# Layer 0's forward transform on sums and differences of halves, and layer 1 without a hand-written order of issue

## The chip, the cores and the metric

The kernel runs on one NeuronCore of one Trainium2 chip, written in Bass with the Tile framework: pools hand out buffers, a planner sets the waits and, where no order is written by hand, the order of the instructions on each engine. The metric is device time in microseconds; less is better. The engines are called PE (matrix products; PEld is its loading of weights), DVE (vector), ACT (activations), POOL (GpSimd) and SP (it only issues DMAs here). All data are float32. In this kernel each matmul of the source appears as two PE instructions in the profile.

## The reference, cut to what matters

x has 16 images of 16 channels, 256x256. Two layers are added to it one after the other, each behind a group normalization with 8 groups (two channels each).

```python
def _L0_conv_ref(x, ty, tx, weights_pole1, weights_pole2, weights_residue):
    alpha = jnp.fft.fft2(x, axes=(-2, -1))
    ...
    A = 1.0 / (omega1[:, None, None, None] - weights_pole1[None])
    Bm = 1.0 / (omega2[:, None, None, None] - weights_pole2[None])
    S = jnp.einsum('ikpq,oikp,xikq->oxik', weights_residue, A, Bm)
    output_residue1 = jnp.einsum('biox,oxik->bkox', alpha, S)
    C = jnp.einsum('biox,oikp->bikpx', alpha, A)
    D = jnp.einsum('bikpx,xikq->bikpq', C, Bm)
    output_residue2 = jnp.einsum('bikpq,ikpq->bkpq', D, weights_residue)
    x1 = jnp.fft.ifft2(output_residue1, s=(Ny, Nx), axes=(-2, -1)).real
    ...
    return x1 + x2 / Nx / Ny

def _L1_conv_ref(x, W1, b1, Wred, bred, Wspan, bspan, W2, b2, Weca):
    f = mish(conv2d(xs, W1, b1))                  # each channel alone, 1 -> 4 maps, 3x3
    top, bot = (f[:, :, :H2], f[:, :, H2:])
    ker = conv2d(jax.nn.relu(conv2d(bot, Wred, bred)), Wspan, bspan)
    ...
    top_inv = (patches * ker[:, None]).sum(axis=2)  # involution of the upper half
    ...
    out = mish(conv2d(shuffled, W2, b2))          # 64 -> 16 maps, 3x3
    pooled = out.mean(axis=(2, 3))
    ...
    return x * gate[:, :, None, None]

x = x + _L0_conv_ref(_gn(x), ...)
x = x + _L1_conv_ref(_gn(x), ...)
return x
```

## The kernel before

Four stages run one after the other, and only DRAM tensors pass between them.

**Layer 0 forward** (`layer0_forward`, from L69). Tables `at`, `bt` (the poles' transforms), `cr`, `ci` (the residues) are built first (L91 to L139). Then for each image `b`, four groups `cg` of four channels: load 1 MB of pixels as `z`, with row halves `h` side by side (L156), statistics on DVE (`bn_stats`), `group_norm_scalars` (two tiny matmuls with `ones`, a chain of small DVE operations, one square root on ACT), and normalization of `z` in place, half of it on DVE, half on POOL (L171). For each channel and column half `xh`, PE makes the row transform `pu` (L180: frequencies 0 to 131, real and imaginary, 264 columns, two row halves accumulated) and `pv` (L194: the product with the pole table, 192 columns). `pu` is copied to `u` by ACT and DVE (L190, L192), `pv` to `v` by ACT (L201), then four products with `bt` give `pd` (L204), which DVE and POOL gather with the residues into `acc` (L214 to L219). After the four groups, the column transform of the image follows: for 33 groups of four frequencies, four matmuls `px` (L233) of 64 weight columns and 512 moving columns; ACT and DVE copy `px` to `o`, POOL issues the store to `al` (L246), whose layout is [33, 64, image, 2, 256].

**Layer 0 mix** (`layer0_mix`) loads `al` one frequency group at a time (L371, SP queue), builds the transfer function `s` (L424), multiplies it with all images (L443), and transforms back along one axis (L470) to `hd`. **Layer 0 back** (`layer0_back`) finishes the inverse transform (L606), adds it to x, normalizes for layer 1, and writes `xp` and the padded `zn`.

**Layer 1** (`layer1`). An image is cut into nine units (j, h): eight of 30 rows by 8 channels and a tail of 4 channels at a time (`blocks`). A unit does, in the class `Unit`: `lower` (conv1 of the lower half, L740; mish to `bot`, L758), `reduce` (1x1 products `pr`, L768; ReLU to `r`, L776; stores of `bot`), `upper(0)`, `upper(1)` (conv1 of the upper half, 16 mish pieces into `wide`, L788), `spread` (eight POOL copies, L800 and L801), `involution(f)` for four maps f (two matmuls `pd`, L808; DVE products and sums, L816 and L819), and stores of `top`. `conv2` of the image before runs at the same time, 48 matmuls in two halves with one PSUM buffer `c2ps` (L882), each closed by a mish with a running sum (L891). `gate` closes an image (L897 to L920): a sum, a tiny matmul, an exponential on ACT (which needs another function table), and four pieces of output that SP loads (`o`, three buffers), POOL scales and stores. `pr`, `pd` and the gate's product share three PSUM buffers (`psd`); conv1 has two.

Layer 1's order on PE, ACT, DVE and POOL is written by hand: `manual_schedule` takes the instructions as the program gives them. A round i handles the next unit's lower, reduce, upper and spread, and between them this unit's four involutions and the two halves of one conv2; rows for a conv2 are asked for one round ahead (`conv2_rows`):

```python
            if nxt:
                nxt.lower()
            if now:
                now.involution(0)
            next(second, None)
            if nxt:
                nxt.reduce()
            if now:
                now.involution(1)
```

All other stages are ordered by the planner. DMAs of POOL are issued in POOL's queue between its other work, those of SP in SP's.

Of the kernel before, what the change touches and what calls it, by code (L numbers as in the profile page):

```python
# [16 lines left out]
C = 16  # L17
N = 256
# [50 lines left out]
def layer0_forward(ctx, tc, d, al, bd):  # L69


    nc = tc.nc
    nb = d["x"].shape[0]
    cp = ctx.enter_context(tc.tile_pool(name="fc", bufs=1))
    sm = ctx.enter_context(tc.tile_pool(name="fs", bufs=2))
    wx = load(nc, cp, d["wx"], [P, 2, 3, N], "wx")
    wxn = load(nc, cp, d["wxn"], [P, 2, 2, 512], "wxn")
    fy = load(nc, cp, d["fy"], [P, 2, 8 * NF], "fy")
    ones = load(nc, cp, d["ones"], [P, P], "ones")

    at = cp.tile([P, 2, C, 3, 64], F32, name="at")
    bt = cp.tile([P, 2, C, 3, 64], F32, name="bt")

    cr = cp.tile([P, C, P], F32, name="cr")
    ci = cp.tile([P, C, P], F32, name="ci")

    with tc.tile_pool(name="fa", bufs=1) as ap, tc.tile_pool(name="fap", bufs=2, space=PSUM) as pp:
        kcol = load(nc, ap, d["kcol"], [P, 2], "kcol")
        for t, axis, planes in ((at, "1", (1, 0, 2)), (bt, "2", (1, 2, 0))):
# [18 lines left out]
            for y in range(2):  # L108
                for half in range(2):
                    cols = slice(512 * half, 512 * half + 512)  # L110
                    for out, terms in ((0, ((0, 0), (2, 1))), (1, ((0, 1), (1, 0)))):
# [12 lines left out]
                        if out == 0:  # L124
                            nc.scalar.copy(dst[:, :, planes[0]], src)
                        else:
                            nc.scalar.copy(dst[:, :, planes[1]], src)
                            nc.vector.tensor_scalar(dst[:, :, planes[2]], src, -1.0, None, ALU.mult)
        mk = load(nc, ap, d["mk"], [P, C], "mk")
        mkb = mk.unsqueeze(1).unsqueeze(3).to_broadcast([P, C, C, M])  # L130
        for t, name in ((cr, "rr"), (ci, "ri")):
            r = ap.tile([P, C, M], F32, tag="res", name=f"res_{name}")
            for a in range(2):
                nc.sync.dma_start(out=r[64 * a : 64 * a + 64], in_=d[f"{name}_kp"])
            rb = r.unsqueeze(2).to_broadcast([P, C, C, M])
            for part in range(2):
                o = t[:, :, 64 * part : 64 * part + 64].rearrange("p i (k q) -> p i k q", q=M)
                nc.vector.tensor_tensor(o, mkb, rb, ALU.mult)
# [3 lines left out]
    up = ctx.enter_context(tc.tile_pool(name="fu", bufs=1))  # L142
# [4 lines left out]
    psv = ctx.enter_context(tc.tile_pool(name="psv", bufs=1, space=PSUM))  # L147
    psx = ctx.enter_context(tc.tile_pool(name="psx", bufs=2, space=PSUM))

    for b in range(nb):  # L150

        u = up.tile([P, 2, 2, NF, 2, 4, 8], F32, tag="u", name="u")
        acc = dp.tile([P, 4, P], F32, tag="acc", name="acc")
        for cg in range(4):
            z = xp.tile([P, 4, 2, N], F32, tag="z", name="z")
            nc.sync.dma_start(  # L156
                out=z.rearrange("p c h x -> p (c h) x"),
                in_=d["x"][b, 4 * cg : 4 * cg + 4].rearrange("c (h p) x -> p (c h) x", p=P),
            )
            mv = sm.tile([P, 2, 2], F32, tag="mv", name="mv")  # L160
            st = sm.tile([P, 4, 6], F32, tag="st", name="st")
            for c in range(4):
                nc.vector.bn_stats(st[:, c], z[:, c].rearrange("p h x -> p (h x)"))
            for g in range(2):
                nc.vector.bn_aggr(mv[:, g], st[:, 2 * g : 2 * g + 2].rearrange("p c s -> p (c s)"))
            nm = sm.tile([P, 2], F32, tag="nm", name="nm")
            rs = sm.tile([P, 2], F32, tag="rs", name="rs")
            group_norm_scalars(nc, sm, psv, ones, mv, 2, nm, rs)
            for g, eng in ((0, nc.vector), (1, nc.gpsimd)):
                zg = z[:, 2 * g : 2 * g + 2]  # L170
                eng.tensor_scalar(zg, zg, nm[:, g : g + 1], rs[:, g : g + 1], ALU.add, ALU.mult)  # L171
            pd = psv.tile([P, 4, P], F32, tag="pd", name="pd")
            for c in range(4):
                ch = 4 * cg + c
                v = vp.tile([P, 2, 3, 64], F32, tag="v", name="v")
                pv = psv.tile([P, 2, 192], F32, tag="pv", name="pv")
                for xh in range(2):
                    pu = psu.tile([P, 2, 4 * NF], F32, tag="pu", name="pu")
                    for yh in range(2):
                        nc.tensor.matmul(  # L180
                            pu.rearrange("p l f -> p (l f)"),
                            lhsT=z[:, c, yh, P * xh : P * xh + P],
                            rhs=fy[:, yh],
                            start=yh == 0,
                            stop=yh == 1,
                        )
                    dst = u[:, xh, :, :, ch // 8, :, ch % 8]
                    src = pu.rearrange("p l (g f) -> p l g f", f=4)
                    if xh == 0:
                        nc.scalar.copy(dst, src)  # L190
                    else:
                        nc.vector.tensor_copy(dst, src)  # L192
                    for yh in range(2):
                        nc.tensor.matmul(  # L194
                            pv[:, xh],
                            lhsT=z[:, c, yh, P * xh : P * xh + P],
# [966 lines left out]
```

## Time and profile before

| what | value |
|---|---|
| median of 3 runs (lowest, highest) | 11,036.04 us (11,033.31, 11,036.97) |
| the profiled execution: its time, its span | 11,036.97 us, 11,035.1 us |
| forward: first matmul of a group norm, first `pu`, first and last start of `px` | 117.3, 126.1, 200.9, 2,262.4 us |
| mix: first `ps`, last start of `ph` | 2,379.5, 5,652.8 us |
| back: first `py`, last start of `py` | 5,851.5, 6,680.3 us |
| layer 1: first conv1, last `c2ps` | 6,706.6, 11,004.9 us |
| busy in all: PE, DVE, ACT, POOL | 9,866.8, 4,483.4, 3,222.3, 2,977.2 us |
| forward's PE rows: `pu`, `pv`, `pd`, `px` | 562.6, 428.4, 273.6, 969.7 us |
| layer 1's PE rows: `c2ps`, `c`, `pd`, `pr` (full units) | 1,423.0, 1,039.8, 1,024.3, 283.8 us |
| granted PE clock, mean | 0.883 |

A row of the profile names the line, the engine, the operation, what it writes and reads, the shape and the number of instructions; then busy time and the mean of one in ns; then the idle time of the engine ahead of the row and what ended it. For PE, `128*64 128x512` is a weight tile of 128 rows and 64 columns and 512 moving columns. [...] the spacing of starts says what it costs in a stream, and busy time counts overlapping instructions once.

### The profile page before, as it was taken

What the parts mean: (1) busy time and instruction counts of PE and PEld (TensorE: products, weight loads), DVE (VectorE), ACT (ScalarE), POOL (GpSimd) and SP (SyncE); (2) the same over time, 40 slices, a digit from 0 to 9 for tenths busy, and PEclk for the clock granted to TensorE, in tenths of its full rate; (3) what the DMA queues carried; (4) which work ended last, traced back from release to release, by engine and by line L of the source; (5) the groups of instructions that cost most, each with busy time, mean ns of one, the idle gap of its engine ahead of it and who ended that gap; (6) DMA issues with size and microseconds to landing.
All of it is one profiled execution on the core that took longest, in us unless ns stands there. A gap on an engine that the chain in (4) does not pass through costs nothing.

```text
span 11035.1 us, 141924 instructions
## 1 busy us (share of the span) xinstructions
PE 9866.8 (89%) x56576; PEld 5619.0 (51%) x56576; DVE 4483.4 (41%) x7653; ACT 3222.3 (29%) x5154; POOL 2977.2 (27%) x3757
## 2 busy tenths in 40 slices
PE   7999999969999999999948997988888888888887
PEld 4666666647666776677636773322222222222222
DVE  4333333242221222212156665555555555555553
ACT  1111111111111111111110114555555555555553
POOL 1111111111111111111101223444444444444443
PEclk9999999977777777777768998999999999999999
DMA  1222222221222212222208996677777777777776
GB/s 59 63 67 66 64 64 66 55 41 36 45 47 47 40 39 46 47 45 38 42 21 274 325 326 182 196 217 220 221 219 216 212 219 216 213 220 214 215 220 199
DMA packets 985862, 1478.78 MB, mean 134 GB/s; under 512 B 74906, under 2 KB 846294, under 8 KB 953078
## 3 DMA queue, kind: packets, MB, share of 16 engines
q1 hardware_dynamic: 848406, 928.46, 31.6%
q0 software_dynamic: 136800, 541.23, 15.1%
q8 instruction: 453, 7.42, 0.3%
q14 instruction: 203, 1.66, 0.1%
HBM read 860.70 MB, written 608.70 MB: 133 GB/s over the span
## 4 chain that ended last, share of the span: by engine, by line
PE 83%; DMA 5%; DVE 5%; issue 3%; ACT 2%; POOL 1%; SPq 0%; ACTq 0%; POOLq 0%; DVEq 0%
PE pg L443 13%; PE c2ps L882 12%; PE px L233 9%; PE pd L808 8%; PE ph L470 8%; PE c L740 8%; PE ps L424 5%; PE pu L180 4%; PE py L606 4%; PE pv L194 3%; PE py L609 2%; PE pd L204 2%; DMA rows<-cf 2%; PE pr L768 2%; DMA z<-zn 1%
## 5 line engine op out<-in xcount | busy, mean ns | idle before, releaser
L788 ACT ACTIVATE wide<-c,b 32x512 f32<-32x512 f32 x2176 | 1477.4, 679 | 480.6 <-PE c L740 429.4
L882 PE MATMUL c2ps<-rows,c 128*32 128x512 f32 x12288 | 1423.0, 611 | 156.4 <-DMA rows<-cf 142.6
L819 DVE TENSOR_TENSOR top<-pd,t 32x512 f32<-32x512 f32 x2176 | 1504.2, 691 | 52.5
L816 DVE TENSOR_TENSOR t<-pd,r 64x512 f32<-64x512 f32 x1088 | 744.0, 684 | 1817.4 <-PE pd L808 1795.0
L443 PE MATMUL pg<-s,alb 128*64 128x32 f32 x16896 | 1407.2, 350 | 1.7 <-issue 1.7
L443 PEld LDWEIGHTS pg<-s,alb 128*64 128x64 f32 x16896 | 1402.1, 272 | 10.6 <-issue 7.8
L808 PE MATMUL pd<-wide,dw 128*128 128x512 f32 x2048 | 1024.3, 623 | 156.5 <-POOL wide L801 155.4
L740 PE MATMUL c<-z,w 102*128 102x512 f32 x2048 | 1039.8, 639 | 112.2 <-ACT wide L788 89.4
L800 POOL COPY wide<-wide 32x1031 f32<-32x1031 f32 (+1 forms) x576 | 569.0, 988 | 1812.7 <-ACT wide L788 1785.2
L882 PEld LDWEIGHTS c2ps<-rows,c 128*32 128x32 f32 x12288 | 391.1, 111 | 1166.4 <-issue 901.3
L233 PE MATMUL px<-wxn,u 128*64 128x512 f32 x4224 | 969.7, 599 | 0.0
L470 PE MATMUL ph<-ix,yt 128*128 128x512 f32 x2112 | 955.3, 605 | 6.7 <-ACT yt L465 5.9
L488 POOL DMA_DIRECT2D hd<-h x512 | 271.9, 535 | 2338.0 <-ACT h L478 2242.1
L424 PE MATMUL ps<-tt,lt 128*64 128x256 f32 x4224 | 659.0, 423 | 156.5 <-DVE lt L410 123.6
L808 PEld LDWEIGHTS pd<-wide,dw 128*128 128x128 f32 x2048 | 376.6, 195 | 782.6 <-issue 435.5
L740 PEld LDWEIGHTS c<-z,w 102*128 102x128 f32 x2048 | 395.1, 195 | 652.3 <-issue 508.4
L233 PEld LDWEIGHTS px<-wxn,u 128*64 128x64 f32 x4224 | 382.8, 136 | 564.2 <-issue 562.3
L470 PEld LDWEIGHTS ph<-ix,yt 128*128 128x128 f32 x2112 | 395.4, 193 | 517.5 <-issue 435.1
L451 DVE COPY y<-pg 128x512 f32<-128x512 f32 x132 | 116.6, 883 | 1224.2 <-PE pg L443 1224.2
L180 PE MATMUL pu<-fy,z 128*128 128x264 f32 x2048 | 562.6, 399 | 35.6 <-DVE z L171 17.8
L801 POOL COPY wide<-wide 32x1031 f32<-32x1031 f32 (+1 forms) x576 | 572.5, 994 | 36.0
L606 PE MATMUL py<-h,iy 128*128 128x256 f32 x2048 | 541.5, 383 | 1.0 <-DMA h<-hd 1.0
(204 smaller groups left out, 9851.0 us busy)
## 6 DMA issues: line engine op xcount, KB each, us to landing
rows<-cf SPq DMA_DIRECT2D x128, 2176.0 KB
z<-zn SPq DMA_DIRECT2D x768, 256.0 KB
cf<-top POOLq DMA_DIRECT2D x512, 240.0 KB, 6.8
cf<-bot POOLq DMA_DIRECT2D x96, 840.0 KB, 9.2
alb<-al SPq DMA_DIRECT2D x528, 128.0 KB
zn<-zb SPq DMA_DIRECT2D x128, 516.0 KB
z<-in_x SPq DMA_DIRECT2D x64, 1024.0 KB
al<-o POOLq DMA_DIRECT2D x256, 256.0 KB, 3.7
```

What stands on the lines that cost most here:

```text
L180: nc.tensor.matmul(pu.rearrange("p l f -> p (l f)"), lhsT=z[:, c, yh, P * xh : P * xh + P], rhs=fy[:, yh], start=yh == 0, stop=yh == 1,)
L233: nc.tensor.matmul(ps[64 * k : 64 * k + 64], lhsT=u[:, xh, part, g0 + j + k].rearrange("p h f c -> p (h f c)"), rhs=wxn[:, xh, part], star ...
L424: nc.tensor.matmul(ps[64 * h : 64 * h + 64, v], lhsT=lt[:, h, v, k], rhs=tt[:, h, k], start=True, stop=True,)
L443: nc.tensor.matmul(ps[64 * h : 64 * h + J, f], lhsT=alv[:, :, fx], rhs=sv[:, :, fx], start=True, stop=True,)
L470: nc.tensor.matmul(ph, lhsT=yt[:, v, h], rhs=ix[:, h, v], start=n == 0, stop=n == 3,)
L606: nc.tensor.matmul(py[:, yh], lhsT=iy[:, v, ys], rhs=h[:, k, v], start=v == 0, stop=False)
L740: nc.tensor.matmul(ps[:, q], lhsT=w, rhs=cols[:, 1 - q], start=True, stop=True)
L788: nc.scalar.activation(self.feat[64 - 32 * q : 96 - 32 * q, f, self.groups[g], :H], ps[32 * f : 32 * f + 32, q], AF.Mish, bias=b1[0][32 * ...
L808: nc.tensor.matmul(ps, lhsT=dwt if self.tail else dw, rhs=self.feat[:, f, cs, :H], start=True, stop=True,)
L816: nc.vector.tensor_tensor(t[64:128], ps[:64], self.r[:, cs], ALU.mult)
L819: nc.vector.tensor_tensor(self.top[32 * f : 32 * f + 32, cs, q], ps[lanes], t[lanes], ALU.add)
L882: nc.tensor.matmul(ps[32 * j : 32 * j + 32], lhsT=c2[:, blk, dx, :], rhs=t[:, 4 * j + blk : 4 * j + blk + 4, x : x + H], start=(blk, dx) = ...
```

## The change

It has two parts.

**Forward.** A group of four channels becomes a step of a pipeline. `halves(b, cg)` loads and makes statistics as before, but instead of normalizing it forms, with the mean taken out, the sum of the two row halves (`eo[:, 0]`, DVE) and their difference (`eo[:, 1]`, POOL). Even row frequencies need only the sum and odd ones only the difference, so `rows` computes each from 128 rows instead of 256: `pu` and `pv` are 128 columns each, one after the other on the same weights. The same is done with the column halves: ACT copies the right half's `pu`, DVE adds and subtracts (two operations a channel) into `u`, so that `columns` makes even and odd column frequencies from 128 columns each, 256 moving columns instead of 512. The scale of the norm is put in when ACT copies `pv` and `px` (all `px` copies are ACT's). `pd` gathers two channels at a time on 64 partitions each; `finish` folds the halves with six small matmuls (`pair`). `halves` of the next group is called ahead of `rows`, and eight groups of `columns` of the image before after each `rows`; `u` has two fixed buffers. `al` has the layout [33, 2, 64, image, 256], its stores are twice as many and half as long, and its loads in the mix take whole pieces. The tables `fy`, `wxn`, `ix`, `krow_t` are reordered to even before odd.

**Layer 1.** The class and the hand-written order are gone. `unit` does one unit's work in its natural order, `conv2` asks for its own rows and runs whole after it, the stores of `top` come before those of `bot`, and the planner sets the order of all engines.

```diff
+    def halves(b, cg):
...
+        eo = ep.tile([P, 2, 4, N], F32, tag="eo", name="eo")
+        for g in range(2):
+            cs = slice(2 * g, 2 * g + 2)
+            nc.vector.scalar_tensor_tensor(
+                eo[:, 0, cs], z[:, cs, 0], nm2[:, g : g + 1], z[:, cs, 1], ALU.add, ALU.add
             )
+        nc.gpsimd.tensor_tensor(eo[:, 1], z[:, :, 0], z[:, :, 1], ALU.subtract)
+        return eo, rs
+
+    def rows(b, cg, eo, rs, acc):
...
+                        lhs = eo[:, e, 2 * j + a, P * xh : P * xh + P]
                         nc.tensor.matmul(
+                            pu[:, xh, e].rearrange("p v m -> p (v m)"),
+                            lhsT=lhs,
+                            rhs=fy[:, e],
+                            start=True,
+                            stop=True,
+                        )
...
+                            pv[:, a, xh],
+                            lhsT=lhs,
+                            rhs=at[:, e, ch].rearrange("p l m -> p (l m)"),
...
+                nc.scalar.copy(right, pu[:, 1])
+                for h, sign in ((0, ALU.add), (1, ALU.subtract)):
+                    nc.vector.tensor_tensor(
+                        u[:, h, :, :64, :, ch],
+                        pu[:, 0].rearrange("p e v m -> p v m e"),
+                        right.rearrange("p e v m -> p v m e"),
+                        sign,
+                    )
+            vt = vp.tile([P, 2, 2, P], F32, tag="v", name="v")
+            nc.scalar.activation(vt, pv, AF.Copy, scale=rs[:, j : j + 1])
...
                     nc.tensor.matmul(
-                        pd[:, c],
-                        lhsT=v[:, xh, 1 - k : 3 - k].rearrange("p l m -> p (l m)"),
+                        pd[64 * a : 64 * a + 64, j],
+                        lhsT=vt[:, a, xh, 64 * k : 64 * k + 64],
...
+    def columns(b, g0, rsc):
...
                         nc.tensor.matmul(
-                            ps[64 * k : 64 * k + 64],
-                            lhsT=u[:, xh, part, g0 + j + k].rearrange("p h f c -> p (h f c)"),
-                            rhs=wxn[:, xh, part],
-                            start=i == 0,
-                            stop=i == 3,
+                            ps[64 * k : 64 * k + 64, :, h],
+                            lhsT=u[:, h, part, g0 + j + k].rearrange("p f c -> p (f c)"),
+                            rhs=wxn[:, h, part],
+                            start=part == 0,
+                            stop=part == 1,
                         )
...
+            for v in range(2):
                 nc.gpsimd.dma_start(
-                    out=al[g0 + k : g0 + n : 2, :, b].rearrange("g p v x -> p g (v x)"),
-                    in_=o[64 * k : 64 * k + 64, :w],
+                    out=al[g0 + k : g0 + n : 2, v, :, b].rearrange("g p x -> p g x"),
+                    in_=o[64 * k : 64 * k + 64, :w, v],
                 )
+
+
+    steps = [(b, cg) for b in range(nb) for cg in range(4)]
+    ready = halves(*steps[0])
+    rsc = None
+    for i, (b, cg) in enumerate(steps):
+        now = ready
+        if i + 1 < len(steps):
+            ready = halves(*steps[i + 1])
+        if cg == 0:
+            acc = dp.tile([P, 2, P], F32, tag="acc", name="acc")
+        rows(b, cg, *now, acc)
+        if b:
+            for g0 in range(8 * cg, 8 * cg + 8 if cg < 3 else NF, 4):
+                columns(b - 1, g0, rsc)
+        if cg == 3:
+            rsc = finish(b, acc)
+    for g0 in range(0, NF, 4):
+        columns(nb - 1, g0, rsc)
...
-                    nc.sync.dma_start(out=alb[p : p + 8, j], in_=al[g, q : q + 8, :, v])
+                    q = 16 * j + 8 * h
+                    nc.sync.dma_start(out=alb[p : p + 8, j], in_=al[g, v, q : q + 8])
...
-    with tc.manual_schedule(engines={E.PE, E.Activation, E.DVE, E.Pool}):
-        begin_unit(0)
-        begin_unit(1)
...
-            if nxt:
-                nxt.lower()
-            if now:
-                now.involution(0)
-            next(second, None)
-            if nxt:
-                nxt.reduce()
...
+    i = 0
+    for b in range(nb + 1):
+        if b:
+            acc = sm.tile([P, 16], F32, tag="acc", name="acc")
+        for s, (j, h) in enumerate(blocks):
+            if b < nb:
+                unit(b, i, j, h)
+                i += 1
             if b and s < 8:
...
+                conv2(b - 1, s, acc)
+        if b:
+            gate(b - 1, acc)
```

## The prediction

> **What bounds the kernel now.** I read the page's first two parts, then busy time by stage (the stretches), then the instruction timeline of one steady piece of each changed stage, and last the waits. All of it says that TensorE (PE) sets the end, in every stage.
>
> ```profile
> PE 9866.8 (89%) x56576; PEld 5619.0 (51%) x56576; DVE 4483.4 (41%) x7653; ACT 3222.3 (29%) x5154; POOL 2977.2 (27%) x3757
> ...
> PE 83%; DMA 5%; DVE 5%; issue 3%; ACT 2%; POOL 1%; SPq 0%; ACTq 0%; POOLq 0%; DVEq 0%
> ```
>
> The stretches (columns: PE, PEld, DVE, ACT, POOL busy, granted clock, DMA share, GB/s): a piece of layer 0's forward stage, the gap after it, a piece of the mix, a piece of layer 1.
>
> ```profile
> 1400.00:2200.00 800.00, 774.07 (x3990) 516.61 (x3989) 248.65 (x618) 140.32 (x270) 152.91 (x174) 0.99 0.23 63
> ...
> 2263.00:2380.00 117.00, 33.19 (x131) 26.88 (x130) 77.02 (x48) 9.95 (x17) 12.90 (x8) 0.65 0.20 37
> ...
> 3000.00:4000.00 1000.00, 950.45 (x7435) 688.30 (x7435) 226.43 (x343) 157.70 (x280) 146.68 (x203) 0.75 0.22 43
> ...
> 8000.00:9000.00 1000.00, 888.95 (x4298) 302.62 (x4302) 538.04 (x802) 524.93 (x782) 440.82 (x571) 0.95 0.71 214
> ```
>
> The forward stage is PE 97% at clock 0.99, other engines under a third: work taken off PE there shortens it. Its size is seen in PE's timeline (start, length, count):
>
> ```profile
> 1000.31 1.07 PE L233 MATMUL px<-wxn,u 128*64 128x512 f32 x2
> 1001.31 1.16 PE L204 MATMUL pd<-bt,v 128*128 128x128 f32 x8
> 1002.40 33.91 PE L233 MATMUL px<-wxn,u 128*64 128x512 f32 x150
> ```
>
> The 150 px follow one another at 33.91/150 = 0.226 us, the 128-column pd at (1.16-0.275)/7 = 0.127. Every matmul of the source is two instructions, each with a weight load.
>
> Layer 1 is one round of 27.88 us per unit (ACT's first r of a round stands at 8307.86, 8335.74, 8363.63), and inside a round PE has no hole over 0.8 us. One line each from the timelines of ACT, POOL and DVE follows one unit from its mish to the first product of its involution; the square brackets hold the idle time before and who ended it:
>
> ```profile
> 8313.46 11.24 ACT L788 ACTIVATE wide<-c,b 32x512 f32<-32x512 f32 x16 [3.09 <-PE c L740]
> ```
> ```profile
> 8319.91 1.03 POOL L800 COPY wide<-wide 32x1031 f32<-32x1031 f32 x1 [15.67 <-ACT wide L788]
> ```
> ```profile
> 8323.33 0.68 DVE L816 TENSOR_TENSOR t<-pd,r 64x512 f32<-64x512 f32 x1 [4.03 <-PE pd L808]
> ```
>
> One unit's own chain is conv1, mish, POOL copies, pd, DVE; with DVE's eight tiles it is longer than a round. It is hidden only because PE works on two units and on conv2 at once. PE's timeline near the end of the kernel shows what a wait costs beyond its length: 24 conv2 calls (48 instructions) take 5.44 us, and 7.10 after PE had stood for 3.03.
>
> ```profile
> 10926.53 7.10 PE L882 MATMUL c2ps<-rows,c 128*32 128x512 f32 x48 [3.03 <-DMA rows<-cf]
> 10934.59 5.44 PE L882 MATMUL c2ps<-rows,c 128*32 128x512 f32 x48 [0.95 <-ACT e L891]
> ```
>
> [...] Here 3.03 us did (7.10 against 5.44), 2.95 us at 10942.98 did not (5.44). [...]
>
> **The change, part 1: forward.** It runs in 64 steps of four channels. PE per step: pu and pv are 64 instructions of 128 columns in place of 264 and 192; nearest rows are pd (0.127) and the 128x128 transposes (8 in 1.05 us, 0.131), so 0.134: 8.6 us. Bounds 0.107 (pv's 192 columns take 0.161 back to back; by columns) and 0.190 (the weight load's own duration). pd: 32 instructions with 64-wide weights, 0.08 from L443 (0.083 apart), bounds 0.067 and 0.137: 2.6. px: 66 on average, 256 columns, 0.12 from L424 (94 in 11.32 us), bounds 0.113 and 0.150: 7.9. Norm matmuls 0.6. Sum 19.7. Before: 2,135 us over 64 steps, 33.4.
>
> Other engines per step. DVE: bn_stats 4x0.68, small norm operations 2.9, the even half 2x0.65 (L105's 1.22 halved), eight u sums of 256 strided elements at 0.60 (L192; bounds 0.41 of L215 and 1.04), pd out 0.9: 12.6, up to 16. ACT: four copies 0.38, two v 0.6, four px 0.6, 5.3. POOL: the odd half 2.5 (twice L219's 1.27 for 512), acc 1.3, 8.5 al DMAs at 0.60 (twice as many), 8.9. None reaches 19.7, so all are hidden under PE; without that cover DVE's 16 would be the bound. The odd half is queued behind the al DMAs, which wait for ACT's last px copies; it is needed a step later, so that costs nothing.
>
> Waits that PE gets: its order puts gn_var after four matmul calls, DVE answers gn_mean with five operations, 0.5 us late; behind gn_var stand all pu. v is read 0.15 and 0.8 late (ACT copies `right` first). [...] So 21.7 a step. The setup keeps its 126 us (fewer table operations, one table loaded twice, in the shade of DVE). 126 + 4 steps without px, held by DVE, x14.5 + 60x21.7 + the last 132 px calls (32) = 1,518 against 2,263: -745. The mix reads al in whole 128 KB pieces; PE waits for that load nowhere now (L443: 1.7 us in all): nothing. al's writes have rows of half the length; DMA share 0.23 leaves room.
>
> **Part 2: layer 1.** The diff takes the order written by hand away and leaves it to the planner. The changed kernel as built has, for each steady unit on PE: lower conv1 (8 instructions), pr, upper conv1, 20 conv2 calls, three pd, then conv2 and single pd in turn, 11 conv2. From the unit's start: lower 0 to 3.6 (0.45 each), second bot ends 4.9 on ACT, its pr 5.9, wide starts 2.06 after the upper conv1 does, 7.96. POOL follows 6.45 later (8313.46 to 8319.91), a pair of copies 2.2: 16.6. PE has done its 20 conv2 (0.227 each) at 14.0: it stands 2.75 us. pd 16.75, DVE 1.17 later, 17.9. psd has three buffers, so the eighth pd waits until DVE has done its fifth tile, 5x2.15 (0.72 for t, 1.43 for two tops): 28.65; pd and sending 1.0, 11 conv2 2.5: 32.15. Against 27.88: +4.3. What else moves is covered. The tops' stores stand on POOL after the unit's copies, now ahead of the bots', and wait for DVE's last tile, 2.95 us into the next unit; with 3.1 of issuing they end at 6.1, and POOL's next copy is not due before 14.4. On SP the rows of a conv2 follow its own unit's z and wait for the conv2 two earlier, so they are issued at the start of the unit before and have a whole round for the 12 to 15 us that they take now (12.70 from 6927.12, 14.77 from 7192.43).
>
> Boundary of a batch. Before: 266.4 a batch (gates at 8499.5 and 8766.0), so 71.2 for tail plus first unit. After, from the tail's first conv1: its last pd 13.6, gate's exponential 19.5, mish's table back 20.9; only then the next bot, whose conv1 was done at 16.8. Rows for the next conv2 wait for the tail's last stores (22, landing 25), then 12 us: 37. SP has them ahead of the fourth o and the next z; z is needed later. 37 conv2 at a cold clock end at 47.9, seven DVE-paced tiles and the next lower at 61.9; that is a unit's start at about 57.5. A batch: 7x32.15 + 57.5 = 282.6, +16.2. Fifteen: +243. Batch 0 has no conv2: 26.75 against 24.4 a unit, +19. The last conv2 start later, +10. Clock: the 2.75 us wait is at the edge; 0 to 1.66 a unit, of which DVE's pace hides a part, 0.3 over 120 units: +35. Sum +307.
>
> Total, against the profiled execution's 11,037.0 (span 11,035.1; the median of the three runs is 11,036.0, the same within 0.01%): 11,037 - 745 + 307 = 10,599.
>
> **The rivals.** (A) Weight loads don't overlap at short streams: 0.190 and 0.137 for all, so 64x0.190 + 98x0.137 + 0.6 = 26.2 a step with the waits hidden under it, 4.5x60 = 270 more than forecast: 10,870. Against: pd's 0.127 with the same weights. (B) Layer 1 loses nothing: the psd waits are absorbed, -745 alone: 10,290. For it: PE's work per round is 26.4 in both. Against: PE's order. (C) Slower: in layer 1 the clock falls at each wait. Place: the pr, pd and e waits of each unit; price 1.66 each. It decides from a unit of 36.1 us, where 15x(8x36.1+25.3-266.4)+29 = 745. Three falls a unit give 37.1: +865, 11,160. Against: 0.8 and 0.95 us waits cool nothing now. That the change does not lessen forward work is excluded by the matmul shapes in its build.
>
> **How the numbers follow.** Forecast 0.66, its own range 10,420 to 10,790 (forward waits 1.5 a step either way 90, boundary 6 a batch 90, clock 0 to 150). A 0.14, B 0.13, C 0.07. The range 10,270 to 10,890 holds the forecast and the better part of A and B. Within 0.2% (22 us, about what a measurement of this kernel can tell from no change) only by accident between A and C: 0.01; slower 0.07; faster 0.92.
>
> **What would show it.** Forward ending near 1,520, PE about 90% busy, pu and pv 0.13 apart; else A. Layer-1 rounds of 32 us, PE waiting 2 to 3 us for POOL before the first pd and idling for DVE before later ones; 28 us would be B. Clock in layer 1 at 0.9 or more; under 0.8 is C. I am wrong if DVE's u sums take over 1.5 us, or if the mix changes.

## The result and the profile after

The changed kernel takes 11,296.31 us (median of 4 runs, 11,290.09 to 11,306.25); the kernel before, run beside it, 11,036.51 us (11,033.31 to 11,037.51). The ratio is 1.0237 (95% interval 1.0219 to 1.0254): 2.4% slower. The forecast was 10,599 us. The profiled execution has a span of 11,304.4 us against 11,035.1, that is +269, and the two traces split it by stage:

| stage, from and to | before | after | difference | forecast |
|---|---|---|---|---|
| start to the last start of `px` | 2,262.8 | 1,370.0 | -893 | -745 |
| last `px` to first `ps` | 116.7 | 110.7 | -6 | 0 |
| mix, first `ps` to last `ph` | 3,273.8 | 3,476.1 | +202 | 0 |
| back with the gaps around it, to the first conv1 | 1,053.3 | 1,053.2 | 0 | 0 |
| layer 1, first conv1 to the end | 4,328.5 | 5,294.4 | +966 | +307 |

The forward stage gave more than was forecast. The mix, for which the forecast had nothing, and layer 1 ate it and more.

The page of the kernel after, its first part and the engines' shares of the chain that ended last:

```profile
PE 9843.9 (87%) x56768; PEld 5331.7 (47%) x56768; DVE 4424.0 (39%) x7953; ACT 3209.6 (28%) x5170; POOL 3142.1 (28%) x4031
...
PE 69%; ACT 10%; DMA 7%; DVE 6%; issue 4%; POOL 4%; SPq 0%; ACTq 0%; POOLq 0%; DVEq 0%
```

PE's busy time is almost what it was (9,866.8), though the forward stage has 815 us less of it (1,318 where 2,133 were). So PE got busier elsewhere at the same number of calls, or spends busy time standing. Its share of the chain fell from 83% to 69%; ACT and DMA have come in. The stretches of the kernel after (PE, PEld, DVE, ACT, POOL busy, granted clock, DMA share, GB/s), one each from forward, mix and layer 1:

```profile
700.00:1300.00 600.00, 600.00 (x5172) 508.31 (x5170) 293.94 (x930) 178.40 (x352) 272.17 (x353) 1.00 0.39 106
2100.00:3100.00 1000.00, 911.73 (x6847) 643.57 (x6845) 211.69 (x321) 149.35 (x267) 139.18 (x194) 0.74 0.22 41
8000.00:9000.00 1000.00, 860.12 (x3410) 241.45 (x3410) 435.74 (x655) 415.54 (x621) 359.26 (x465) 0.93 0.61 174
```

Forward: PE 100% at clock 1.00, nothing else over half. Mix: PE 912 us of 1,000 where it was 950. Layer 1: 3,410 matmul instructions in 1,000 us where there were 4,298, yet PE is still 86% busy, and the clock is 0.93 in the mean (0.95 before). PE does a fifth less there in nearly the same busy time. That is the thing to explain.

**Forward.** PE's timeline inside a step, in the kernel after (start, length, count):

```profile
715.20 0.39 PE L204 MATMUL pu<-fy,eo 128*128 128x128 f32 x2
715.42 0.39 PE L211 MATMUL pv<-at,eo 128*128 128x128 f32 x2
...
717.14 1.58 PE L232 MATMUL pd<-bt,v 128*64 128x128 f32 x16
...
723.89 7.41 PE L288 MATMUL px<-wxn,u 128*64 128x256 f32 x58
```

Read starts, not lengths: two `pu` instructions are 0.39 us long, but to the next two `pv` it is 0.22, so 0.11 each; the 16 `pd` end where the next `pu` starts (718.65), 0.094 each; the 58 `px` run to 731.23, 0.127 each. A step (712.22 to 731.47) is 19.25 us, with no wait in it.

**Layer 1.** The same three marks of one unit as were shown of before, in the timelines of ACT, POOL and DVE of the kernel after:

```profile
8310.91 11.26 ACT L853 ACTIVATE wide<-c,b 32x512 f32<-32x512 f32 x16 [1.36 <-PE c L817]
```
```profile
8317.37 1.03 POOL L863 COPY wide<-wide 32x1031 f32<-32x1031 f32 x1 [8.83 <-ACT wide L853]
```
```profile
8320.72 0.69 DVE L872 TENSOR_TENSOR t<-pd,r 64x512 f32<-64x512 f32 x1 [17.57 <-PE pd L868]
```

The chain from mish to DVE is as long as before (9.8 us, where it was 9.9), but DVE has now been idle for 17.57 us ahead of it: the next unit's front no longer runs beside this unit's back. PE's timeline of the rest of the unit, which starts at 8302.13 and ends at 8339.84, 37.72 us in all where the forecast had 32.15:

```profile
8319.56 4.50 PE L868 MATMUL pd<-wide,dw 128*128 128x512 f32 x6 [2.44 <-POOL wide L864]
8323.99 1.05 PE L934 MATMUL c2ps<-rows,c 128*32 128x512 f32 x2
8324.97 1.13 PE L868 MATMUL pd<-wide,dw 128*128 128x512 f32 x2
8326.02 1.06 PE L934 MATMUL c2ps<-rows,c 128*32 128x512 f32 x6
8328.04 1.05 PE L934 MATMUL c2ps<-rows,c 128*32 128x512 f32 x2 [0.95 <-ACT e L943]
...
8330.07 1.07 PE L934 MATMUL c2ps<-rows,c 128*32 128x512 f32 x8
...
8332.13 1.94 PE L934 MATMUL c2ps<-rows,c 128*32 128x512 f32 x12
...
8335.05 1.05 PE L934 MATMUL c2ps<-rows,c 128*32 128x512 f32 x4
...
8337.09 2.81 PE L934 MATMUL c2ps<-rows,c 128*32 128x512 f32 x22
```

Two instructions are one conv2 call. One call takes 0.98 us to the start of what follows (mostly a `pd`; most of their rows are left out), four 1.00, six 1.87, two 0.99, eleven 2.75; three, ahead of a wait, are 1.06 long. The price goes by fours begun, some 0.95 each, not by calls. In a stream (40 instructions at 8312.54 in 4.57 us) a call is 0.23, four of them 0.91. Four calls in a row write the four groups of 32 output rows (`ps[32 * j : 32 * j + 32]`) with weights of 32 columns each, and run side by side: the stream's first four instructions start from 8312.54 to 8312.56, the next four from 8313.01 to 8313.03 (run 11 shows it for conv2 and `pr`). The planner puts a `pd` (128 weight columns) after 20, 21, 25, 29, 35 and 37 of the unit's 48 calls. A piece that is no multiple of four takes the time of the next whole four: by time the unit has 15 fours, where 48 calls need 12. Over the kernel the same 12,288 instructions are busy for 1,835.7 us, where they were for 1,423.0:

```profile
L934 PE MATMUL c2ps<-rows,c 128*32 128x512 f32 x12288 | 1835.7, 613 | 186.8 <-ACT e L943 174.3
```

A second thing is hidden in the mean of the clock. The first three `pd` of the unit take 4.43 us. Two stretches of 1 us show why (the columns as above; the clock is the last but two):

```profile
8321.00:8322.00 1.00, 1.00 (x2) 0.25 (x1) 0.96 (x2) 0.97 (x2) 0.94 (x2) 0.50 0.26 52
...
8324.00:8325.00 1.00, 1.00 (x4) 0.16 (x3) 0.87 (x2) 0.00 (x0) 0.99 (x1) 1.00 0.00 0
```

From 8320.59, 1 us behind the end of the 2.44 us wait, the granted clock is 0.5 for 3.41 us. The records of the clock have a fall at this place in 104 of 118 full units with a conv2; PE then takes 20.3 us (median) from the first `pd` to the next unit. In four units that had the wait and kept their clock it takes 19.1. So the fall costs 1.2 us a unit, some 125 us in all by an estimate from these figures. In the kernel before, the clock is 1.00 throughout the rounds that the forecast quotes (from 8307.86 to 8363.63).

**Mix.** The costliest group of ACT there and PE's `ph`, in the kernel before and after, then one unit of the mix on ACT and on PE in the kernel after:

```profile
L478 ACT COPY h<-ph 128x512 f32<-128x512 f32 x264 | 154.7, 586 | 847.9 <-PE ph L470 736.0 <-DMA hd<-h 94.5 <-PE pt L459 17.4
L470 PE MATMUL ph<-ix,yt 128*128 128x512 f32 x2112 | 955.3, 605 | 6.7 <-ACT yt L465 5.9 <-DVE yt L467 0.7
```
```profile
L555 ACT COPY h<-ph 128x512 f32<-128x512 f32 x264 | 154.7, 586 | 1050.8 <-PE ph L547 746.1 <-DMA hd<-h 304.7
L547 PE MATMUL ph<-ix,yt 128*128 128x512 f32 x2112 | 1026.0, 639 | 134.6 <-ACT yt L542 133.9 <-DVE yt L544 0.7
```
```profile
2319.90 0.58 ACT L555 COPY h<-ph 128x512 f32<-128x512 f32 x1 [8.74 <-DMA hd<-h]
```
```profile
2320.81 9.23 PE L547 MATMUL ph<-ix,yt 128*128 128x512 f32 x14 [4.30 <-ACT yt L542]
```

ACT waits 305 us in all for a store of `h` to land (94.5 before); `yt` is queued behind that on ACT, and PE's `ph` waits for `yt`: 134 us in the open (5.9 before), while its busy time is 71 longer (1,026.0 against 955.3). That makes 199 of the 202. The records of single transfers show what is new: the loads of `alb` come in pieces of 16 KB that take 1.8 us each (median over the mix), where they were 1 KB and 0.10. Stores of `h`, in pieces of 4 KB and 0.3 us as before, go out in the middle of them: the four issued from 2,295 to 2,310 us landed 16.4 us later (median). Of all 544 such stores 181 took more than 12 us to land, where 19 had before. The others land sooner than before, so the median over all, 3.4 us against 6.7, does not show it.

So the theory was: the three stages add up independently; layer 1 loses by broken fours of conv2, the mix by the new layout of `al`. The rivals: that layer 1's loss comes in part from the new layer 0, that it is the changing between two kinds of matmul that costs, or that DVE or POOL set the round; and for the mix, that the new order of rows or the clock is to blame. The expectations of the runs on layer 1's order do not reckon with the fall of the clock; the traces of runs 6, 7 and 9 have it too, and are read for it there.

### The profile page after: what moved, and what is told of

It reads as the page before. It is cut to its first block, busy times and chain, and to the rows that moved or that the text cites. A ratio compares the mean times of both kernels' runs of the same rounds, so it can differ in the third digit from the quotient of the medians.

```text
span 11304.4 us, 142231 instructions
## 1 busy us (share of the span) xinstructions
PE 9843.9 (87%) x56768; PEld 5331.7 (47%) x56768; DVE 4424.0 (39%) x7953; ACT 3209.6 (28%) x5170; POOL 3142.1 (28%) x4031
## 3 DMA queue, kind: packets, MB, share of 16 engines
q0 software_dynamic: 141152, 541.25, 16.3%
## 4 chain that ended last, share of the span: by engine, by line
PE 69%; ACT 10%; DMA 7%; DVE 6%; issue 4%; POOL 4%; SPq 0%; ACTq 0%; POOLq 0%; DVEq 0%
PE pg L520 12%; PE pd L868 9%; PE c2ps L934 8%; ACT wide L853 8%; PE ph L547 6%; PE c L817 6%; PE ps L501 5%; PE px L288 5%; DMA hd<-h 5%; PE py L683 4%; PE pu L204 2%; PE pr L837 2%; PE py L686 2%; PE pv L211 2%; DMA o<-xp 2%
## 5 line engine op out<-in xcount | busy, mean ns | idle before, releaser
L934 PE MATMUL c2ps<-rows,c 128*32 128x512 f32 x12288 | 1835.7, 613 | 186.8 <-ACT e L943 174.3
L868 PE MATMUL pd<-wide,dw 128*128 128x512 f32 x2048 | 1277.4, 737 | 385.0 <-POOL wide L864 377.8
L547 PE MATMUL ph<-ix,yt 128*128 128x512 f32 x2112 | 1026.0, 639 | 134.6 <-ACT yt L542 133.9
L817 PE MATMUL c<-z,w 102*128 102x512 f32 x2048 | 1026.0, 641 | 22.5 <-DMA z<-zn 22.5
L943 ACT ACTIVATE e<-c2ps,b 128x512 f32<-128x512 f32 x256 | 175.9, 687 | 2151.4 <-PE c2ps L934 2151.0
L547 PEld LDWEIGHTS ph<-ix,yt 128*128 128x128 f32 x2112 | 418.3, 205 | 692.8 <-issue 475.6
L886 POOL DMA_DIRECT2D cf<-top x512 | 257.1, 502 | 1646.8 <-DVE top L875 1619.9
L288 PE MATMUL px<-wxn,u 128*64 128x256 f32 x4224 | 580.3, 386 | 0.0
```

The source lines that it names most:

```text
L288: nc.tensor.matmul(ps[64 * k : 64 * k + 64, :, h], lhsT=u[:, h, part, g0 + j + k].rearrange("p f c -> p (f c)"), rhs=wxn[:, h, part], star ...
L547: nc.tensor.matmul(ph, lhsT=yt[:, v, h], rhs=ix[:, h, v], start=n == 0, stop=n == 3,)
L817: nc.tensor.matmul(ps[:, q], lhsT=w, rhs=cols[:, 1 - q], start=True, stop=True)
L868: nc.tensor.matmul(ps, lhsT=dwt if tail else dw, rhs=feat[:, f, cs, :H], start=True, stop=True)
L934: nc.tensor.matmul(ps[32 * j : 32 * j + 32], lhsT=c2[:, blk, dx, :], rhs=t[:, 4 * j + blk : 4 * j + blk + 4, x : x + H], start=(blk, dx) = ...
```

## The experiments

**1. The new layer 0 alone.** The changed `layer0_forward`, `layer0_mix`, tables and layout, with the function `layer1` of before:

```diff
-            if b < nb:
-                unit(b, i, j, h)
...
+    with tc.manual_schedule(engines={E.PE, E.Activation, E.DVE, E.Pool}):
+        begin_unit(0)
```

> The changed layer 0 (forward, tables, layout of al) with the hand-ordered layer 1 of before. Theory (the parts add up): the traces show the forward 893 us shorter, the mix some 200 us longer and layer 1 966 us longer; without the last, 11,036 - 893 + 200 = about 10,345 us. Rival (part of layer 1's loss comes from what the new layer 0 leaves behind, a lower clock for instance): layer 1 stays longer than its 4,328 us, and the time lies between 10,400 and 11,300.

Measured: 10,358.96 us, ratio 0.9369 (0.9355 to 0.9383). Its mix is 3,496 us long, its layer 1 4,328, exactly as before.

**2. The new layer 1 alone.** The other way round: all of layer 0 as before, and

```diff
-    with tc.manual_schedule(engines={E.PE, E.Activation, E.DVE, E.Pool}):
-        begin_unit(0)
...
+            if b < nb:
+                unit(b, i, j, h)
```

> The layer 0 of before with the changed layer 1 (the order left to the planner). Theory: all of layer 1's loss, about 966 us, so 12,000 us, with a unit's round of 37.7 us instead of 27.9. Rival (part of it belongs to the new layer 0): clearly under 12,000.

Measured: 12,038.01 us, ratio 1.0886 (1.0870 to 1.0902). Layer 1 is 5,308 us (5,294 in the changed kernel), the steady batch 327.7 us (327.5). The parts add up (0.9369 and 1.0886 make 1.0255, against 1.0237); nothing of layer 1's loss belongs to the new layer 0.

**3 and 4. Two cures for the mix**, both on the kernel of run 1. The old layout of `al` under the new arithmetic (the stores of `al` in the forward, left out here, are again half as many and twice as long):

```diff
-    al = dram.tile([NF, 2, 64, nb, N], F32, name="al")
+    al = dram.tile([NF, 64, nb, 2, N], F32, name="al")
...
-                    nc.sync.dma_start(out=alb[p : p + 8, j], in_=al[g, v, q : q + 8])
+                    nc.sync.dma_start(out=alb[p : p + 8, j], in_=al[g, q : q + 8, :, v])
```

> As the kernel with the changed layer 0 and the old layer 1, but al keeps its old layout, frequency by row by image by part, so that each load of alb is 128 pieces of 1 KB again; the arithmetic is the changed one. Theory (the new layout makes the alb loads hold up the hd stores, so h buffers come free late and ACT, yt and ph wait): the mix goes back to some 3,273 us, so 10,140 to 10,160, about 200 below the run with the new layout; ACT's wait for hd falls from some 305 us to under 100. Rival (the mix lost its 200 us elsewhere, by the new order of rows and tables or by a lower clock): no difference, 10,345.

And, with the new layout kept, more buffers for `h`:

```diff
+    hb = ctx.enter_context(tc.tile_pool(name="mhh", bufs=8))
...
-            o = hp.tile([P, 2, N], F32, tag="h", name="h")
+            o = hb.tile([P, 2, N], F32, tag="h", name="h")
```

> As the kernel with the changed layer 0 and the old layer 1, new layout of al kept, but 8 buffers for h in the mix instead of 3. Theory (stores land late, and only the three buffers turn that into a wait): ACT's wait for hd goes and the time falls to about 10,140 to 10,160, as with the old layout, or a little lower since before had 94 us of that wait too. Rival A (the loads hold up something other than the h buffers): no difference to the run with three, 10,345. Rival B (the mix lost its time elsewhere): no difference either, and the run with the old layout does not differ either.

Measured: 10,148.94 us, ratio 0.9178 (0.9163 to 0.9193), and 10,152.26 us, ratio 0.9180 (0.9166 to 0.9194). ACT's row in the first and in the second:

```profile
L554 ACT COPY h<-ph 128x512 f32<-128x512 f32 x264 | 154.8, 586 | 854.6 <-PE ph L546 717.2 <-DMA hd<-h 130.3 <-PE pt L535 7.1
```
```profile
L556 ACT COPY h<-ph 128x512 f32<-128x512 f32 x264 | 154.8, 586 | 822.4 <-PE ph L548 800.6 <-DMA hd<-h 21.8
```

Either cure alone brings the mix back (3,294 and 3,289 us; with the old layer 0, in run 2 beside them, it is 3,294). PE's own wait for `yt` is 5.0 us and nothing. The loss needs both: stores that land late, and only three buffers behind them. The records of the stores agree: over 12 us to land took 23 of them with the old layout, and 201 with eight buffers, where they no longer hold up PE. Order of rows and tables are those of the changed kernel in both runs, so they are not the cause.

**5. Both cures together**, the two diffs above in one kernel.

> The changed forward, al in its old layout, 8 buffers for h in the mix and the hand-ordered layer 1 of before: the two cures of the mix together. If the wait for h buffers that is left with the old layout (130 us on ACT) still stands on the path, some tens of us under 10,149, down to 10,050; if the path through the mix is TensorE's by then, the same 10,149.

Measured: 10,129.90 us, ratio 0.9177 (0.9162 to 0.9193): the same as either alone. So the 130 us that ACT waits for `hd` with the old layout are off the path, but for some 17 us at most, which the interval leaves open.

**6. The control for layer 1.** Layer 0 of before; the planner's order on PE written out by hand, so that the cuts of conv2 can be moved. Numbers are conv2 calls before the first `pd` and behind each of the eight:

```diff
+    cuts = [20, 0, 0, 1, 4, 4, 6, 2, 11]
...
+            calls(cuts[0])
+            for f in range(4):
+                for g in range(2):
+                    if now:
+                        now.involution(f, g)
+                    calls(cuts[1 + 2 * f + g])
```

> Layer 0 of before; layer 1 in an order written by hand that copies the planner's on TensorE call by call: the unit's c and pr, 20 conv2 calls, three pd, then conv2 in pieces of 1, 3 and 1, 4, 6, 2 and 11 calls with a pd between each two. It is the control. Theory (TensorE's order alone costs the time): 12,038 us, as with the planner's own order, unit 37.7. Rival (the planner's order on the other engines or queues has a share in it): faster by more than 100 us.

Measured: 12,276.68 us, ratio 1.1122 (1.1106 to 1.1139). The unit is the planner's, 37.75 us, with the same pieces at the same prices. The total misses by 239 us (some 260 by the ratios). At the start of each batch PE waits some 20 us for conv2's rows (338 us in all, nothing in run 2); that this order has no front work left to put there is my reading, not tried. The next two runs share that wait (336 and 330), so they are compared with this one, and not with the totals expected. The fall of the clock is shared by run 7 as well: 88 of 119 units here, 84 there.

**7. Cuts only at whole fours.**

```diff
-    cuts = [20, 0, 0, 1, 4, 4, 6, 2, 11]
+    cuts = [20, 0, 0, 4, 4, 4, 8, 0, 8]
```

> As the control, but conv2 is cut only at multiples of four calls (20, three pd, then pieces of 4, 4, 4, 8 and 8 with the pd between). Theory (four conv2 calls to the four groups of 32 columns run side by side, so that a broken four takes as long as a whole one, 0.95 us): 15 fours by time become 12 a unit, 3 x 0.95 = 2.85 us less, times 128 units: 365 us less than the control, 11,670, unit 34.9. Rival A (what costs is each change between conv2 and pd): two changes fewer of twelve, so at most 60 us less. Rival B (DVE's five or POOL's copies set the round): no difference.

Measured: 11,815.20 us, ratio 1.0704 (1.0688 to 1.0720), 461 less than the control. The rows of conv2 in the control and here:

```profile
L882 PE MATMUL c2ps<-rows,c 128*32 128x512 f32 x12288 | 1871.4, 614 | 467.1 <-DMA rows<-cf 338.0 <-ACT e L893 124.0 <-DVE top L819 5.0
```
```profile
L882 PE MATMUL c2ps<-rows,c 128*32 128x512 f32 x12288 | 1529.6, 617 | 352.4 <-DMA rows<-cf 336.4 <-ACT e L893 16.1
```

The same 12,288 instructions are busy for 342 us less: 2.67 a unit against the 2.85 expected of three fours. The rest is a second effect of the cuts that I had not separated: the control starts the second half right behind the first one's last call and waits 0.95 us for ACT to empty the one PSUM buffer (124 us); here a `pd` stands between, and that wait is gone (16). 342 and 108 make 450 of the 461. The unit shown is 33.73 us, and in it DVE works through its eight tiles without a gap.

DVE does not set this round, though. Here are the first three `pd` of that unit and of the next one, which is 32.55 us long:

```profile
9032.76 4.39 PE L808 MATMUL pd<-wide,dw 128*128 128x512 f32 x6 [2.44 <-POOL wide L801]
...
9066.48 1.98 PE L808 MATMUL pd<-wide,dw 128*128 128x512 f32 x4 [2.43 <-POOL wide L801]
9068.67 1.12 PE L808 MATMUL pd<-wide,dw 128*128 128x512 f32 x2 [0.21 <-POOL wide L801]
```

The waits differ by 0.01 us, but in the first unit the clock falls to 0.5 behind it and in the second it stays at 1.00: 4.32 us to the next conv2 call against 3.25. Over the run PE takes 16.3 us from the first `pd` to the next unit with the fall (84 units), and 15.1 in 21 without. The 21 had waits of 2.35 us and more as well. What decides between two equal waits was not found.

**8. Conv2 not cut at all.**

```diff
-    cuts = [20, 0, 0, 1, 4, 4, 6, 2, 11]
+    cuts = [24, 0, 0, 0, 0, 0, 0, 0, 24]
```

> As the control, but conv2 is not cut: 24 calls, all eight pd, 24 calls. Theory: the fours stay whole, but TensorE now stands while DVE works off the pd: first pd 17.4 us into the unit (POOL), DVE frees the buffer for the eighth 1.2 + 5 x 2.09 later, pd 1.0, 24 calls 5.5: unit 35.5, so about 11,760, between the other two. Rival A (the changes cost): far fewer of them, so it is the fastest of the three, under 11,600. Rival B (DVE or POOL sets the round): at or above the control.

Measured: 12,161.32 us, ratio 1.1019 (1.1003 to 1.1035), 115 less than the control; the unit is 35.82 us (35.5 expected). Of the 400 us above the total expected, 239 are the control's own; the rest was not followed. The fours are whole (1,453.7 us busy), and PE now shows DVE's pace in the open:

```profile
9126.17 1.10 PE L808 MATMUL pd<-wide,dw 128*128 128x512 f32 x2 [1.05 <-DVE top L819]
9128.31 1.10 PE L808 MATMUL pd<-wide,dw 128*128 128x512 f32 x2 [1.05 <-DVE top L819]
```

A `pd` every 2.14 us, one DVE tile each. Few cuts are not the aim: conv2 has to fill these holes, in whole fours. By the rival of the changing itself this run would be the fastest of the three, under 11,600 us; that is refuted.

**9. The third `pd`.** In run 7 three `pd` take 4.4 us, I thought because the third needs POOL's second pair of copies. Four calls are put ahead of it:

```diff
-    cuts = [20, 0, 0, 4, 4, 4, 8, 0, 8]
+    cuts = [20, 0, 4, 0, 4, 4, 8, 0, 8]
```

> As the run with cuts at multiples of four, but the four calls behind the third pd are put in front of it. In that run the third pd stands at the head of TensorE's queue until POOL has made the second map's two copies: three pd take 4.4 us from the first's start, where three back to back would take 2.7. Theory: the four calls (0.95 us) now fill that hole, so the third pd and all behind it come as they did and the 0.95 us falls away, times 128 units: 120 us less, ratio to before 1.060 instead of 1.070. Rival (DVE's chain of eight tiles sets the round, so filling TensorE's hole gains nothing): 1.070.

Measured: 11,826.31 us, ratio 1.0698 (1.0680 to 1.0716): no difference. The rival gave the number, but the trace does not bear out its reason. DVE never waits over 0.25 us from the first `t` at 9035.42 to the last at 9050.66, yet here too the units without a fall of the clock are shorter at the same pace of DVE: 14.9 us from the first `pd` to the next unit in 19 of them, 16.3 in 86 with the fall (15.1 and 16.3 in run 7). The hole was mostly the slow clock. The wait for POOL in it is 0.21 us by run 7's second unit above, and filling it gains 0.2; where the clock falls, the four calls run at 0.5 themselves and take 1.86 us instead of 1.00:

```profile
9036.84 1.94 PE L882 MATMUL c2ps<-rows,c 128*32 128x512 f32 x8
9038.70 2.04 PE L808 MATMUL pd<-wide,dw 128*128 128x512 f32 x4
```

Whether an order without the wait of 2.44 us would keep the clock up and gain the 1.2 us was not tried.

**10 and 11. The cuts put into the kernel before.** Its own order, and in each half of conv2 one `pd` between the calls, 4 calls from the edge in the first run (shown, for the first half) and 2 in the second:

```diff
-            if now:
-                now.involution(0)
-            next(second, None)
+            if now:
+                now.involution(0, (0,))
+            calls(4)
+            if now:
+                now.involution(0, (1,))
+            calls(20)
```

> The kernel before, its layer 1 in its own order, with one edit: in each half of conv2 one pd is put between the calls, behind the 4th of the first half and in front of the last 4 of the second. Theory (only broken fours cost): the fours stay whole, two more stretches of conv2 a unit; by the control's trace a change costs some 0.07 us, four of them x 128 units = 35 us: 11,075 us. Rival [...]: some 250 us more, 11,290.

> The same two pd, put behind the 2nd call of the first half and in front of the last 2 of the second: as many changes, but each half now has a piece of 2 and one of 22 calls, 7 fours by time instead of 6. Theory: 2 x 0.95 us a unit more than the run with pieces of 4 and 20, x 128 units = 243 us, so about 11,320. Rival (the change itself costs): the same time as the run with 4 and 20.

Measured: 11,131.50 us, ratio 1.0089 (1.0075 to 1.0103), and 11,299.01 us, ratio 1.0240 (1.0226 to 1.0254). The difference is 168 us, 1.31 a unit, where two whole fours were expected (1.90), and the cut at 4 costs 97 us where 35 were expected (the rival's 250 was an estimate). PE's timeline of the run with 2 and 22, at the end of a first and of a second half, tells why the first is too small:

```profile
9603.69 0.59 PE L768 MATMUL pr<-bot,wr 128*32 128x512 f32 x1
9603.69 0.59 PE L882 MATMUL c2ps<-rows,c 128*32 128x512 f32 x1
9603.69 0.59 PE L768 MATMUL pr<-bot,wr 128*32 128x512 f32 x1
...
9620.83 1.06 PE L882 MATMUL c2ps<-rows,c 128*32 128x512 f32 x4
```

Behind the first half's 22 calls stands `pr`, which also has 32 weight columns, and its instructions start in the same moment as the last of conv2: they run beside them. So the broken four costs nothing more; but ACT's mish of conv2 now starts as late as the `pr`, and ahead of its `r`, so that the second `pr` waits 1.51 us for ACT, not 0.79 as in run 10. Only where a `pd` follows does the half four cost a whole one (four instructions, two calls, 0.99 us to the next start). This is the most direct sight of matmuls side by side. If the 97 us of the cut at 4 are the price of changing between 32 and 128 weight columns, which no run separates, it is small: 97/128 = 0.76 us for four more changes a unit, 0.19 each (23 of the 97 are a longer wait for conv2's rows).

**12. The forward's interleaving.** On the kernel of run 3, the 33 `columns` of an image in one block after its own rows.

```diff
         rows(b, cg, *now, acc)
-        if b:
-            for g0 in range(8 * cg, 8 * cg + 8 if cg < 3 else NF, 4):
-                columns(b - 1, g0, rsc)
         if cg == 3:
             rsc = finish(b, acc)
+            for g0 in range(0, NF, 4):
+                columns(b, g0, rsc)
```

> The changed forward with al in its old layout and the hand-ordered layer 1 of before, but the 33 column transforms of an image stand in one block behind its own rows instead of between the next image's steps. It does the same arithmetic. Theory (the forward's gain is the halved count of matmul instructions; the placing between steps hides little): TensorE waits once an image for u, 2 to 5 us x 16, and a step without px is 11 us of TensorE against some 9.4 of DVE: 10,180 to 10,230 (10,149 with the placing). Rival (the placing gives the cover, and steps without px are held by DVE at the 14.5 us that my forecast took for them): 64 x 3.5 more, 10,370 or above.

Measured: 10,149.05 us, ratio 0.9199 (0.9187 to 0.9212), against 0.9178 (0.9163 to 0.9193) in run 3; the last `px` starts at 1,388.3 us instead of 1,372.7. So 16 to 23 us at most, at the edge of what is measured, and less than either side expected. The forward's gain is the smaller work on PE, not where the transforms stand.

## Why the prediction failed, step by step

- **Forward, -745 forecast, -893 measured: right mechanism, one term too large.** A step is 19.25 us, not 21.7, and 60 steps of 2.45 are 147 of the difference of 148. The waits taken as 2.0 us (0.5 of them my estimate for POOL's difference, which no trace of before had shown) are not there: four calls of `pu` and `pv` hide the norm's answer, and POOL's difference did not hold up DVE so that PE noticed. `pu` and `pv` cost 0.112, not 0.134 (-1.4 a step); `pd` 0.094 for 0.08 and `px` 0.127 for 0.12 take 0.9 back. Rival A, weight loads that don't overlap, is refuted by the 0.112.
- **"The mix reads al in whole 128 KB pieces; PE waits for that load nowhere now: nothing." Failed: +202.** I asked whether anyone waits for the load, and not whom the load would hold up. The trace shows pieces of 1.8 us where there were 0.10, and four stores issued among them that landed 16.4 us later (median); runs 3 and 4 show that the layout and the three `h` buffers are the cause. That the pieces' size and not another property of the new layout delays the stores fits the records, but was not tried by itself, and by what mechanism the stores are held up was not shown.
- **Layer 1, +307 forecast, +966 measured: the failed step is "11 conv2 2.5" and its like, conv2 at 0.227 a call wherever it stands.** By traces the batches' 14 periods gave +852 (60.8 each, forecast 16.2), the front up to the first gate +122, the end -8. The unit is 37.72, not 32.15. The first `pd` comes 17.43 into the unit, not 16.75. From there to the next unit PE takes 20.3 where the sum has 15.4, and 15.1 in those units of run 7 whose clock does not fall. Runs 6 and 7 give the broken fours and the wait for `e`, which the forecast put at nothing, together 3.9 (three fours of 0.95 are 2.85, the wait 0.95); the clock is the other 1.2. The cuts made PE the pace where I had DVE: DVE waits 0.55, 1.83 and 0.73 us for `pd` inside each unit of the changed kernel.
- **The clock, 0.3 a unit forecast, 1.2 measured: right mechanism, too small.** The forecast had the wait before the first `pd` "at the edge". In the trace of before two waits lie on either side of that edge: after 3.03 us the granted clock was 0.50 (10928 to 10930) and 24 calls took 7.10 us, after 2.95 it was 1.00 (10945 to 10947) and they took 5.44. In the changed kernel it fell at some 2.4 us in 104 of 118 units, though not in the four units that kept their clock, nor at a wait of 2.43 in run 7.
- **The waits I listed are there as forecast**: 2.44 us for POOL before the first `pd` (2.75), in which PE stands although a half of conv2 is begun, whose next call starts only after the three `pd`, at 8323.99; and the unit's own chain, no longer hidden. Batch 0 has 30.5 us a unit where 26.75 were forecast; in it `pr` waits 1.65 us for DVE to free a buffer of `psd`, which is a part of that; the boundary of a batch, where ACT loads the exponential's table and mish's back in 1.28 us each, is 63.5 instead of 57.5. Neither was followed further.
- **The rivals.** B (layer 1 loses nothing) is refuted. C named the right side and nearly the right unit, 37.1, with a mechanism that is a minor part: the clock falls once a unit, not three times, and for 1.2 us, not 1.66 each. That its unit comes so near is luck, for it has no broken fours. Its sign, a mean clock under 0.8, could not show the fall either: the mean is 0.93 with it. That is the lesson of the chances: the side was open because layer 1 had a threshold of 36.1 us, and I had only the clock to cross it.

## What to carry to other kernels

Where calls run side by side, as conv2's four here (0.95 us for a four, whole or broken), cut the stream only at whole groups, or put another narrow matmul into the gap, as `pr` stood in it in run 11. Read the clock inside one round (0.50 for 3.41 us), not as a mean over a stage (0.93). When a layout makes transfers larger (16 KB pieces for 1 KB here), look at which others then land late (181 stores of 544 over 12 us, where 19 were) and at how many buffers stand behind them (three), not only at who waits for the transfer. And two independent changes are worth separating before they are judged: this forward with the old layout of `al` and the old layer 1 takes 10,149 us, 8.2% less than before, hidden in a change that is 2.4% slower.

## What the runs showed of the hardware

- One float32 matmul of 32 weight columns and 512 moving columns (two instructions) takes 0.98 us to the start of the `pd` behind it, and four in a row into different column groups 0.91 to 1.00; in a stream four instructions start within 0.02 us of each other (8312.54) and the next four 0.46 later. A `pr` and a conv2 call into other groups start at the same moment (run 11, 9603.69).
- Four more changes between 32 and 128 weight columns a unit cost 97 us in run 10, at most 0.19 us each (23 of the 97 are a longer wait for rows), far less than a broken four (0.95).
- At a wait of some 2.4 us (2.44 in the unit shown) the granted clock fell to 0.5, mostly for 3.41 us, in 104 of 118 units of the changed kernel, and PE took 1.2 us longer (20.3 where 19.1); at a wait of 2.43 in run 7 it did not fall. After a wait of 24.08 us in run 6 the same 40 conv2 instructions took 6.50 us instead of 4.57.
- With loads in 16 KB pieces in place of 1 KB, 181 of 544 stores of 128 KB took more than 12 us to land, where 19 had; with eight buffers behind them 201 did, at no loss of time.
